# Key scales for the next head: eight loads of 256 KB spread over a head, in place of two of 1 MB

## The chip, the cores and the metric

The kernel runs on one core of one Trainium2 chip. The metric is the device time of one execution in microseconds (us). Before the change three runs took 1708.43, 1709.20 and 1712.97 us, a median of 1709.2 us. The profile comes from one further execution, which took 1714.34 us.

## The reference

The reference is one layer of gated cross attention followed by a gated feed-forward block, with quantisation simulated in both. Cut to what matters here:

```
q = LN(x) @ Wq + bq          # 2048 rows, 16 heads of 32
k, v = ctx @ Wkv + bkv       # 4096 rows
q, k: per row and head   round(x / s) * s,  s = max|x| / 127
v:    per column         round(v / s) * s
attn = softmax(q k^T / sqrt(32))           # 16 heads, 2048 x 4096
attn = round(attn / s) * s,  s = max(attn) / 255   # per row
x = x + tanh(g) * (attn @ v) @ Wp + ...
x = x + tanh(g2) * FFN(LN(x))              # 1.58-bit weights, 512 -> 2048 -> 512
```

All 2048 queries see all 4096 keys. Keys are held as integers, so each column of the score matrix has to be multiplied by its key's scale. These are the *key scales*: for each head one row of 4096 numbers.

## The kernel before, in words

There are three stages. In the first (to about 237 us) rows of x and ctx are normalised, projected and quantised, and the integers and scales go to DRAM: `q4d`, `k4d`, and `skd`, which holds the key scales as 16 rows of 4096 floats. The second stage is the attention loop (237 to 1454 us). The third is the feed-forward block.

**The loop.** A *unit* is one head and 128 queries, and there are 16 heads of 16 units, 256 in all (`steps`). For each unit:

- TensorE (PE) multiplies 128 queries by 4096 keys in three chunks of 1536, 1536 and 1024 (`scores`, L726).
- VectorE (DVE) multiplies each chunk by the key scales, writes it to one of three score buffers and takes the maximum (L735). The scales stand in the tile `skb`, 128 partitions of 4096 floats, every partition the same.
- GpSimd (POOL) makes the exponent's bias from the maximum (L750, L752). ScalarE (ACT) takes the exponential and rounds it to one byte per key (`exps`, L755); the result `r` has three buffers.
- The sync engine's queue (SP) issues a DMA that transposes `r` into `pT` (`turn_exps`, L769). POOL casts the transposed bytes to 16 bits (`rT<-pT`, L789), PE multiplies them by the values (L805), and ACT takes the product out (L816).

**Order.** Every engine runs its instructions in an order that the program writes out by hand (`manual_schedule`). One pass of the loop for unit i issues the scores of unit i, between them the exponentials of unit i-1 and whatever `plan` holds for the place (casts, value products and their loads), and at the end the transpose of unit i-2. After that transpose come the loads for the next head, so all of these stand in SP's one queue, behind and in front of the transposes.

**Loads for the next head.** A head needs three tiles: `kT` (its keys, from `k4d`), `skb` (from `skd`), `qT` (its queries, from `q4d`). Each has two buffers, so a head's tiles are filled while the head before runs. `load_piece(h, n)` issues one of eight pieces: n = 0, 1 are halves of `kT` and n = 4 to 7 quarters of `qT`, as transposing DMAs (L256); n = 2, 3 are halves of `skb`, 1 MB each, one 8 KB row of DRAM read once for each of 128 partitions (L249). In heads 1 to 13 piece n comes at unit 2n, so the scales come at units 4 and 6. In head 0 the places are in `LATE`: pieces 0 to 7 come at units 4, 6, 8, 10, 11, 12, 13 and 14. The last head's pieces are loaded at the start of the last 32 units, which alternate between two heads.

**Values.** For three of the four groups of heads, the values are projected inside the loop (`plan_group`, L652, started at units 3, 64 and 129): their inputs come by loads of 512 KB (`fx<-cTd`, L646), go out to DRAM (`vtd`, L674), come back in loads of 256 KB (`fx<-vtd`, L678) and are transposed (`vq<-fx`, L278). These also stand in SP's queue, mostly in heads 0 to 11.

Of the kernel before, what the change touches and what calls it, by code (L numbers as in the profile page):

```python
# [23 lines left out]
P = 128  # L24
# [9 lines left out]
def flamingo_kernel(  # L34
# [31 lines left out]
    nc = tc.nc  # L66
# [5 lines left out]
    H, HD = 16, 32  # L72
# [43 lines left out]
    KB = 512  # L116
    q4d = dram.tile([NQ, HPG * C], BF16, name="q4d")
    k4d = dram.tile([NK // HPG, HPG * C], BF16, name="k4d")
    skd = dram.tile([H, NK], F32, name="skd")
# [115 lines left out]
    heads = {}  # L235
# [3 lines left out]
    def load_piece(h, n):  # L239
        if h not in heads:  # L240
            heads[h] = (
                ah.tile([P, 1, NK // HPG], BF16, name="kT"),
                ah.tile([P, NK], F32, name="skb"),
                ah.tile([P, 1, NQ], BF16, name="qT"),
            )
        kT, skb, qT = heads[h]
        if n in (2, 3):
            a = (n - 2) * NK // 2
            nc.sync.dma_start(  # L249
                skb[:, a : a + NK // 2],  # L250
                skd[h : h + 1, a : a + NK // 2].broadcast_to([P, NK // 2]),
            )
            return
        dst, src, n = (kT, k4d, n) if n < 2 else (qT, q4d, n - 4)
        a = n * KB
        nc.sync.dma_start_transpose(  # L256
            dst[:, :, a : a + KB], src[a : a + KB, h * P : (h + 1) * P]
        )

    def value_scale(g, vmx):  # L260
# [48 lines left out]
    with tc.tile_pool(name="pw", bufs=1) as pw, tc.tile_pool(  # L309
# [79 lines left out]
        for t in range(QT - END):  # L389
            a = LEAD + 2 * t  # L390
# [159 lines left out]
        with tc.manual_schedule():  # L550
# [9 lines left out]
            n = len(order)  # L560
# [68 lines left out]

    VW = 256  # L630
    NV = NK // VW
    LATE = (4, 6, 8, 10, 11, 12, 13, 14)
    VALUES = {3: (1, 4, 2), 64: (2, 66, 0), 129: (3, 131, 0)}

    def plan_group(g, u0, dense):
# [76 lines left out]
    def scores(i, n):  # L712
        h, t = steps[i]
        kT, skb, qT = heads[h]
        if n == 0:
            live[i] = (
                scores_buffer(i),
                ar.tile([P, len(CHUNKS)], F32, name="m3"),
            )
        s, m3 = live[i]  # L720
        k0, w = CHUNKS[n]
        ps_s = asc.tile([P, CHUNKS[0][1]], F32, name="ps_s")
        for b in range(k0 // KB, (k0 + w) // KB):
            a, r = divmod(b, HPG)
            rows = slice(r * HD, (r + 1) * HD)
            nc.tensor.matmul(  # L726
                ps_s[:, b * KB - k0 : (b + 1) * KB - k0],
                qT[rows, 0, t * P : (t + 1) * P],
                kT[rows, 0, a * KB : (a + 1) * KB],
                start=True,  # L730
                stop=True,
                tile_position=(r * HD, 0),
            )

        nc.vector.tensor_tensor_reduce(  # L735
            s[:, k0 : k0 + w],
            ps_s[:, :w],
            skb[:, k0 : k0 + w],
            1.0,
            -3.0e38,  # L740
            ALU.mult,
            ALU.max,
            m3[:, n : n + 1],
        )

    def exps(i):
        h, t = steps[i]
        s, m3 = live.pop(i)
        m = ar.tile([P, 1], F32, name="m")
        nc.gpsimd.tensor_scalar(m, m3[:, 0:1], m3[:, 1:2], m3[:, 2:3], ALU.max, ALU.max)  # L750
        nb = ar.tile([P, 1], F32, name="nb")
        nc.gpsimd.tensor_scalar(nb, m, nsq[:, t, h : h + 1], LN255, ALU.mult, ALU.add)  # L752

        r = ar.tile([P, NK], U8, name="r")
        nc.scalar.activation(  # L755
            r.rearrange("p (n two) -> p two n", two=2),
            s.rearrange("p (two n) -> p two n", two=2),
            AF.Exp,
            bias=nb,
            scale=sq[:, t, h : h + 1],  # L760
            accum_out=rowsum[:, t, h : h + 1],
        )
        turning[i] = r

    def turn_exps(i):
        h, t = steps[i]
        if t % 2 == 0:
            heads["p", h, t // 2] = at.tile([P, 2, KT // 2, P], I16, name="pT", bufs=5)
        nc.sync.dma_start_transpose(  # L769
            heads["p", h, t // 2][:, t % 2, :, :],  # L770
            turning.pop(i).bitcast(I16),
        )
        if t % TG == TG - 1:
            plan_values(i, h, t // TG)
# [215 lines left out]
    def tiles(g):  # L990
        return range(g * GT, (g + 1) * GT)
# [421 lines left out]
    for j in range(8):  # L1413
        a = j * INNER // 8
# [43 lines left out]
    with tc.manual_schedule():  # L1458
        nc.vector.memset(less, -128.0 * INT_STEP)
        nc.vector.memset(ones_h, 1.0)  # L1460
        for i in range(len(steps)):
            h, t = steps[i]
            for n in range(len(CHUNKS)):
                scores(i, n)

                if n == 0 and i in VALUES:
                    plan_group(*VALUES[i])
                if n == 0 and i:
                    exps(i - 1)
                for run in plan.pop((i, n), ()):  # L1470
                    run()
            if i > 1:
                turn_exps(i - 2)
            if h == 0:
                if t in LATE:
                    load_piece(1, LATE.index(t))
            elif h + 2 < H and t % 2 == 0:
                load_piece(h + 1, t // 2)
            if 0 <= i - PAIR < TG:
                for n in ((0, 4, 2), (1, 3), (5,), (6, 7))[i - PAIR]:  # L1480
                    load_piece(H - 1, n)

        last = len(steps)

        def rest(i, n):
            return plan.pop((i, n), [])

        def run(fs_):  # L1490
            for f in fs_:
                f()

        def spreads_of(i, *engines):

            fs_ = [f for f in plan[i, 2] if isinstance(f, partial)]
            plan[i, 2] = [f for f in plan[i, 2] if not isinstance(f, partial)]
            return [partial(f, cast=e) for f, e in zip(fs_, engines)]

        act, pool = nc.scalar.copy, nc.gpsimd.tensor_copy  # L1500
        turn_exps(last - 2)
        exps(last - 1)
        turn_exps(last - 1)
        run(rest(last - 1, 3))
        for t in tiles(1):
            bias_x(t)
        take_second_head()
        take_scores()
        nc.gpsimd.memset(xis[1][:, :, C:], 0.0)
        for t in tiles(2):  # L1510
            load_x(t)
        run(rest(last, 1))
        run(rest(last + 1, 1))
        integers_x(0)
        for n in range(2, 8):
            first_project(2, n)
        wide_step(3)
        run(spreads_of(last, act, act))
        run(spreads_of(last + 1, pool, pool))
        for t in tiles(0):  # L1520
            turned_x(t)
            turned_x_out(t)
        residual_x(2)
        turned_steps(3)
        scale_o(3)
        take_bytes()
        for t in tiles(2):
            load_o(t)
        for t in tiles(3):
            load_x(t)  # L1530
        for name, v in (("lg", ln_g), ("lb", ln_b)):
            nc.sync.dma_start(vecs[name], row(v, INNER))
        steps_x(2)
        run(rest(last + 2, 1))
        run(spreads_of(last + 2, pool, pool))
        hidden(0, 0)
        run(rest(last + 3, 1))
        project(3)
        hidden(0, 1)
        quarter = spreads_of(last + 3, act, act)  # L1540
        run(rest(last + 3, 2))
        run(quarter[:1])
        residual_x(3)
        factors_x(1)
        integers_x(1)
        for t in tiles(2):
            bias_x(t)
        wide_step(4)
        hidden(1, 0)
        run(rest(last + 4, 1))  # L1550
        run(quarter[1:])
        run(spreads_of(last + 4, pool, pool))
        turned_steps(4)
        hidden(1, 1)
        scale_o(4)
        wide_step(5)
        run(rest(last + 5, 1))
        run(spreads_of(last + 5, act, act))
        project(4)
        turned_x(2)  # L1560
        turned_x_out(2)
        residual_x(4)
        gelu(0)
        turned_steps(5)
        scale_o(5)
        run(rest(last + 6, 1))
        project(5)
        gelu(1)
        bias_y(0)
        variance(0)  # L1570
        variance(1)
        factors_h(0)
        run(rest(last + 7, 1))
        run(rest(last + 7, 2))
        turned_x(3)
        residual_x(5)
        turned_x_out(3)
        factors_x(2)
        bias_y(1)
        for t in tiles(3):  # L1580
            load_o(t)
            bias_x(t)
        steps_x(3)
        take_rest()
        for k in range(2):
            nc.sync.dma_start_transpose(W2[k], w2q[:, k * INNER // 2 : (k + 1) * INNER // 2])
        for t in tiles(3):
            wide_step(t)
        for s in range(1, NGT - 2):
            turn(s)  # L1590
        last_turns()
# [32 lines left out]
```

## Time and profile before

| | |
|---|---|
| median of three runs | 1709.2 us |
| profiled execution, its own time | 1714.34 us |
| its span (first to last instruction) | 1712.5 us |
| attention loop in it | 236.7 to 1454.0 us |
| DVE busy over the span | 1566.7 us, 91% |
| ACT, POOL, PE busy | 1343.1, 1283.7, 1366.1 us |
| loads of key scales (L249) | 32 of 1024 KB |
| DMA busy, mean over the 16 engines, tenths | 9 in nearly every slice of the loop |

How to read it: busy times are of one execution. A group is named by line, engine, operation and tiles (out<-in). "Idle before" is time for which the engine stood still ahead of that group, with what ended it. SP does no arithmetic; its rows in the timeline are the time that it took to issue a DMA, and it takes the next only when that is done. The DMA share is the busy time of packets over that of 16 engines, and can pass 1 where packets overlap.

### The profile page before, as it was taken

To read this page: it belongs to the slowest core of one execution; us is meant where nothing else is said; L and a number is where in the kernel's file an instruction comes from. 1 tells how busy PE (TensorE), PEld (TensorE's weight loads), DVE (VectorE), ACT (ScalarE), POOL (GpSimd) and SP (SyncE) were. 2 spreads that over 40 slices of the span, in tenths; PEclk is the share of its full clock that TensorE was granted. 3 is DMA by queue.
4 is the path that set the end of the run, shared out by engine and by line. 5 is a ranking of instruction groups with operands and counts; after the bars stand their busy time and mean duration, and the time that the engine had idled before them with its cause. 6 is when DMAs were issued, how large, how long until landed. Compare 5 with 4: busy or idle time off the path is not lost. (4 is left out here: it accounts for less than half of the span.)

```text
span 1712.5 us, 31561 instructions
## 1 busy us (share of the span) xinstructions
PE 1366.1 (80%) x12174; PEld 592.1 (35%) x12174; DVE 1566.7 (91%) x2205; ACT 1343.1 (78%) x988; POOL 1283.7 (75%) x1315
## 2 busy tenths in 40 slices
PE   8999968889966899886678998766666577789986
PEld 4444423333322333332233333222222233434432
DVE  5787889999999999999989999999999989578998
ACT  2443468888889798888978888898887877679987
POOL 0001226889999899999988999999999998656645
PEclk9999975555555555555555556555555555889998
DMA  6767969999999999999999999989999776613325
GB/s 208 274 248 249 300 189 225 194 211 212 181 200 189 212 189 207 208 197 202 173 208 185 227 181 215 202 171 198 165 198 179 151 140 130 169 50 87 89 53 117
DMA packets 736331, 315.92 MB, mean 184 GB/s; under 512 B 658034, under 2 KB 703670, under 8 KB 729782
## 3 DMA queue, kind: packets, MB, share of 16 engines
q1 hardware_dynamic: 727414, 309.19, 83.4%
q10 hardware_dynamic: 8736, 4.72, 1.1%
q8 instruction: 95, 1.56, 0.4%
q14 instruction: 54, 0.44, 0.1%
q0 software_dynamic: 32, 0.01, 0.0%
HBM read 110.15 MB, written 40.12 MB: 88 GB/s over the span
## 5 line engine op out<-in xcount | busy, mean ns | idle before, releaser
L789 POOL CAST rT<-pT 128x2048 int16<-128x2048 uint8 x506 | 944.1, 1892 | 28.9 <-DMA pT<-r 7.5
L735 DVE CUSTOM_DVE_ANT_0 s<-ps_s,skb 128x1536 f32<-128x1536 f32 x531 | 806.0, 1574 | 21.1 <-PE ps_s L726 13.0
L755 ACT ACTIVATE r<-s,nb,sq 128x4096 uint8<-128x4096 f32 x177 | 673.1, 3803 | 135.6 <-POOL nb L752 77.1
L726 PE MATMUL ps_s<-kT,qT 32*128 32x512 bf16 x2048 | 463.7, 593 | 245.7 <-DVE m L735 232.1
L735 DVE CUSTOM_DVE_ANT_0 third<-ps_s,skb 128x1536 f32<-128x1536 f32 (+1 forms) x237 | 362.6, 1574 | 5.5 <-PE ps_s L726 3.2
L755 ACT ACTIVATE r<-third,nb,sq 128x4096 uint8<-128x4096 f32 x79 | 300.3, 3802 | 46.7 <-POOL nb L752 34.0
L726 PEld LDWEIGHTS <-qT 32*128 32x128 bf16 x2048 | 95.4, 99 | 578.0 <-issue 571.1
L805 PE MATMUL acc<-rT,vq 128*32 128x128 f16 x8192 | 265.1, 307 | 33.3 <-ACT o L816 25.2
L805 PEld LDWEIGHTS <-vq 128*32 128x32 f16 x8192 | 196.8, 137 | 147.0 <-issue 105.1
L652 PE MATMUL vacc<-fx 128*128 128x256 f32 x384 | 231.4, 706 | 7.7 <-ACT fx L661 6.7
L750 POOL TENSOR_SCALAR m<-m 128x1 f32<-128x1 f32 x256 | 91.8, 359 | 67.8 <-DVE m L735 61.2
L472 POOL TENSOR_SCALAR nsq<-sq 128x16 f32<-128x16 f32 x16 | 3.2, 203 | 171.9 <-DVE sq L291 171.9
L652 PEld LDWEIGHTS vacc<-fx 128*128 128x128 f32 x384 | 94.9, 306 | 91.3 <-issue 79.2
L431 PE MATMUL kacc<-wk_sb,cT 128*128 128x512 f32 x256 | 117.7, 603 | 0.0
L752 POOL TENSOR_SCALAR nb<-m,nsq 128x1 f32<-128x1 f32 x256 | 67.8, 265 | 23.9
L1117 PE MATMUL ph<-fx,skb 128*128 128x512 bf16 x256 | 64.2, 396 | 0.1
L431 PEld LDWEIGHTS kacc<-wk_sb,cT 128*128 128x128 f32 x256 | 47.1, 194 | 47.6 <-issue 47.0
L735 DVE DVE_READ_ACCUMULATOR2_ANT m<- 128x1 f32 x768 | 62.7, 82 | 0.0
L431 PE MATMUL qacc<-wq_sb,xT 128*128 128x512 f32 x128 | 59.4, 608 | 0.1
L460 DVE TENSOR_TENSOR f<-kacc,bk_sb 128x512 f32<-128x512 f32 x32 | 22.0, 689 | 31.1 <-PE kacc L431 30.1
L300 ACT COPY cT<-tr 128x512 f32<-128x512 f32 x32 | 18.6, 580 | 34.8 <-PE tr L299 34.6
L360 POOL TENSOR_SCALAR wi<-wt 128x512 bf16<-128x512 int32 (+1 forms) x32 | 21.7, 704 | 31.5 <-ACT wt L356 19.3
(233 smaller groups left out, 1370.1 us busy)
## 6 DMA issues: line engine op xcount, KB each, us to landing
skb<-skd SPq DMA_DIRECT2D x32, 1024.0 KB
fx<-cTd SPq DMA_DIRECT2D x48, 512.0 KB
wt<-in_L_ffn_w_dram SPq DMA_DIRECT2D x16, 1024.0 KB
in<-in_ctx_dram SPq DMA_DIRECT2D x32, 256.0 KB
cTd<-cT SPq DMA_DIRECT2D x8, 1024.0 KB
q4d<-rows4q SPq DMA_DIRECT2D x16, 512.0 KB
vtd<-fx SPq DMA_DIRECT2D x24, 256.0 KB
fx<-vtd SPq DMA_DIRECT2D x24, 256.0 KB
```

The lines of the kernel that those rows point to most:

```text
L360: nc.gpsimd.tensor_scalar(wi[:, a : a + w4], wt.bitcast(I32)[:, a : a + w4], 1.0, -1.0, ALU.min, ALU.max)
L431: nc.tensor.matmul(acc, tT[:, c, :], wk_sb[c] if kind == "k" else wq_sb[:, c, :], start=(c == 0), stop=(c == CC - 1),)
L460: nc.vector.tensor_tensor(f, acc, bk_sb, ALU.add)
L652: nc.tensor.matmul(state["acc"], wv_g[:, c, :], state["cT", j][:, c, :], start=(c == 0), stop=(c == CC - 1),)
L726: nc.tensor.matmul(ps_s[:, b * KB - k0 : (b + 1) * KB - k0], qT[rows, 0, t * P : (t + 1) * P], kT[rows, 0, a * KB : (a + 1) * KB], start=True,
L735: nc.vector.tensor_tensor_reduce(s[:, k0 : k0 + w], ps_s[:, :w], skb[:, k0 : k0 + w], 1.0, -3.0e38, ALU.mult, ALU.max, m3[:, n : n + 1],)
L750: nc.gpsimd.tensor_scalar(m, m3[:, 0:1], m3[:, 1:2], m3[:, 2:3], ALU.max, ALU.max)
L752: nc.gpsimd.tensor_scalar(nb, m, nsq[:, t, h : h + 1], LN255, ALU.mult, ALU.add)
L755: nc.scalar.activation(r.rearrange("p (n two) -> p two n", two=2), s.rearrange("p (two n) -> p two n", two=2), AF.Exp, bias=nb, scale=sq[: ...
L789: cast(spreads[k][:, 2 * u : 2 * u + 2, :, :] .bitcast(I16) .rearrange("p a (two b) q -> p a two (b q)", two=2), pTs[u][:, :, k * NW : (k ...
L805: nc.tensor.matmul(acc[c * HD : (c + 1) * HD, :], vq[:, kb, h % HPG * HD : (h % HPG + 1) * HD], rT[:, c, b, :], start=(k == 0 and b == 0), ...
L1117: nc.tensor.matmul(ph[:, n, :], xqT[:, c, tok], w1T[:, c, at : at + 512], start=(c == 0), stop=False,)
```

## The change

Two tables take the place of `LATE` and of the rule "piece n at unit 2n". The scales of the next head are loaded in eight pieces of 512 keys (256 KB: 2 KB for each of 128 partitions) by a new function `load_scales`; the pieces of `kT` and `qT` move forward to units 0, 2, 4, 6, 8 and 10. In head 0 everything comes four units later than in the others. The first head's tiles (loaded before the loop) and the last head's are loaded as before, in halves.

```diff
+    def load_scales(h, k):
+        a = k * KB
+        nc.sync.dma_start(
+            heads[h][1][:, a : a + KB], skd[h : h + 1, a : a + KB].broadcast_to([P, KB])
+        )
...
-    LATE = (4, 6, 8, 10, 11, 12, 13, 14)
+    PIECES_AT = {0: (0,), 2: (1,), 4: (4,), 6: (5,), 8: (6,), 10: (7,)}
+    SCALES_AT = {1: (0,), 3: (1,), 5: (2,), 7: (3,), 9: (4, 5), 10: (6,), 11: (7,)}
...
             if i > 1:
                 turn_exps(i - 2)
-            if h == 0:
-                if t in LATE:
-                    load_piece(1, LATE.index(t))
-            elif h + 2 < H and t % 2 == 0:
-                load_piece(h + 1, t // 2)
+            if h + 2 < H:
+                for n in PIECES_AT.get(t if h else t - 4, ()):
+                    load_piece(h + 1, n)
+                for k in SCALES_AT.get(t if h else t - 4, ()):
+                    load_scales(h + 1, k)
```

## The prediction

> **What bounds the kernel now.** I read the page first: which engine is busiest, and in which groups.
>
> ```profile
> PE 1366.1 (80%) x12174; PEld 592.1 (35%) x12174; DVE 1566.7 (91%) x2205; ACT 1343.1 (78%) x988; POOL 1283.7 (75%) x1315
> L735 DVE CUSTOM_DVE_ANT_0 s<-ps_s,skb 128x1536 f32<-128x1536 f32 x531 | 806.0, 1574 | 21.1 <-PE ps_s L726 13.0
> L789 POOL CAST rT<-pT 128x2048 int16<-128x2048 uint8 x506 | 944.1, 1892 | 28.9 <-DMA pT<-r 7.5
> ```
>
> DVE leads, and nearly all of it is the scaling of scores (L735). In the loop DVE runs from one chunk to the next; a unit takes 4.50 us where nothing disturbs it. So the loop can only gain what DVE stands idle. The second view is the table of windows, one per head (I cut at the start of each head's first chunk), of which these are heads 1, 4, 5, 8 and 9:
>
> ```profile
> core 0: us, PE busy (x) PEld busy (x) DVE busy (x) ACT busy (x) POOL busy (x), PEclk, DMA share, GB/s
> 313.50:390.50 77.00, 67.74 (x686) 28.32 (x686) 74.16 (x100) 64.98 (x42) 69.56 (x65) 0.50 1.05 201
> 539.90:618.70 78.80, 64.19 (x677) 27.54 (x675) 74.38 (x102) 64.65 (x42) 69.38 (x64) 0.50 1.02 207
> 618.70:692.90 74.20, 67.83 (x687) 28.62 (x686) 73.74 (x101) 63.31 (x42) 69.70 (x65) 0.50 1.00 200
> 842.60:924.50 81.90, 63.49 (x676) 27.03 (x673) 75.43 (x102) 66.06 (x45) 69.64 (x64) 0.50 0.99 199
> 924.50:998.50 74.00, 66.63 (x682) 28.77 (x682) 73.61 (x99) 64.23 (x39) 69.32 (x64) 0.50 1.05 205
> ```
>
> Length minus DVE busy is DVE's idle time: 2.8 us in head 1, 4.4 in head 4, 6.5 in head 8, but 0.5 and 0.4 in heads 5 and 9. Taken so for heads 0 to 13, the ones in which the change acts, the sum is 19.3 us: 5.8 in heads 0 and 1, 10.9 in heads 4 and 8, 2.6 in the other ten. That is the ceiling of any gain. The DMA share is about 1 throughout: DMA has little room, and a burst delays what is behind it.
>
> Third, what ended DVE's idle time in the loop (list of waits, DVE, us in total, times, longest):
>
> ```profile
> DVE s L735 <- PE ps_s L726: 13.0, 17, 3.1
> DVE s L735 <- ACT r L755: 5.5, 7, 1.9
> DVE vmx L671 <- ACT fx L661: 3.6, 3, 1.5
> ```
>
> PE itself is not short of time, so something holds it. The timeline of the worst place, head 8, shows it engine by engine (start, length, what; idle before it in brackets):
>
> ```profile
> 872.02 1.16 SPq L249 DMA_DIRECT2D skb<-skd  x1
> 873.28 6.48 SPq L769 DMA_TRANSPOSE pT<-r  x1
> ...
> 881.95 3.80 ACT L755 ACTIVATE r<-third,nb,sq 128x4096 uint8<-128x4096 f32 x1 [3.40 <-DMA pT<-r]
> ...
> 887.68 1.23 DVE L735 CUSTOM_DVE_ANT_0 s<-ps_s,skb 128x1024 f32<-128x1024 f32 x1 [3.08 <-PE ps_s L726]
> ...
> 881.97 1.89 POOL L789 CAST rT<-pT 128x2048 int16<-128x2048 uint8 x1 [3.08 <-DMA pT<-r]
> ...
> 886.05 1.05 PE L805 MATMUL acc<-rT,vq 128*32 128x128 f16 x32 [3.59 <-ACT o L816]
> ```
>
> A load of key scales is issued; the transpose behind it takes 6.48 us to issue instead of the usual 3.0 (median of L769). ACT waits 3.4 us for that transpose to free its buffer, POOL 3.1 us for its data, the value product on PE waits for ACT, the next scores stand behind it in PE's order, and DVE stands still for 3.1 us. The packets give the same: for four of those us the engines carry almost only 8 KB packets, some 36 in a us. One load keeps all 16 engines busy for 2.6 to 4.1 us.
>
> **The change part by part.**
>
> *Two loads of 1 MB go, eight of 256 KB come, in each of 14 heads.* The nearest row for the new load is L678, a load of the same 128 x 2 KB from DRAM; L249 is the old one (ns: shortest, median, longest issue):
>
> ```profile
> L249 SPq DMA_DIRECT2D skb<-skd x32: 332/576/1592, 226.8 to 1305.2; - x32
> L678 SPq DMA_DIRECT2D fx<-vtd x24: 424/530/999, 475.2 to 1155.4; - x24
> ```
>
> On the DMA engines: a packet of 2 KB takes 84 ns (median) against 315 for 8 KB; the 128 packets of one L678 load add up to 0.72 to 1.2 us of 16 engines, mostly 0.85. Eight make 6.8 us a head against 2 x 3.5 = 7.0 before. Engine work costs nothing more. On SP: 8 x 0.53 less 2 x 0.58, and 0.1 between any two issues, gives +3.7 us a head, 52 us in all. What hides it: SP's issues fill 1052 of the loop's 1217 us, and most of the rest it waits for ACT to finish r, about 10 us a head. Where that cover is thin (issues fill 70 of 73 us in head 12, 79 of 82 in head 8, and SP runs 4 to 8 us behind ACT from the middle of heads 3 and 7 into 4 and 8), the 3.7 us make it later. Bounds: 0 if the issue lies beside DMA work, which the transposes that stand blocked suggest; 3.7 us in each of heads 3, 7, 8 and 12, 15 us, if it all shows. Nearest to the first, because ACT and POOL can take a transpose some 5.5 us late before DVE stops (three r buffers): I take +2 us.
>
> The Trainium skill, "DMA: Bandwidth & Descriptors", section "Measured (HBM→SBUF, 128 partitions, SWDGE, issued from GpSimd)", says to batch to 1 MB or more, and its fit in "Anatomy of one DMA" is a fixed 2.0 us plus bytes over 436 GB/s. An estimate by it: 20.8 us for eight loads against 8.8 for two, 12 us more a head and 168 us over 14, were they run one at a time (the page's numbers are of DMAs issued by GpSimd; these come from SP). The L678 rows do show about 2.8 us from issue to last byte, so a wait of that kind is there, but the DMAs behind go on meanwhile, and this case's price is the 0.85 us above.
>
> *The burst goes.* A transpose now finds at most about 0.9 us in front of it (1.7 at unit 9) instead of 3.5. In heads 4 and 8 each of the two bursts made ACT wait 3 to 4 us, and the second came before the first was recovered (ACT recovers 4.50 - 4.0 = 0.5 us a unit). I expect DVE to lose 4 us there instead of 10.9, what is left coming from SP's lag at the end of heads 3 and 7: -7 us (bounds 0 and -10.9). In heads 0 and 1 ACT also waits for transposes right after the scale loads (1.7 and 2.6 us in head 0): -3 of 5.8 (bounds 0 and -5.8). In the ten others -1 of 2.6.
>
> *kT and qT pieces move.* The first three `qT` pieces come 4, 4 and 4 units earlier, at units 4, 6 and 8 instead of 8, 10 and 12, the last at 10 instead of 14. Six transposes of 1.25 us a head, same number, no cost of their own. Units 9 to 11 now carry four scale loads and a `qT` piece, about 3.5 us of DMA more than before; units 12 to 15 carry nothing, and let SP catch up for the next head. Free, unless SP is already late there (heads 3 and 7: 3 to 5 us late; +3 would reach the edge of 5.5). Its cost lies within the +2 and +15 above.
>
> *Waits that the change adds.* DVE's first unit of a head now waits for three loads per chunk rather than one; in heads 1 to 13 the last is issued at unit 11, four units ahead, so they are met. Not so out of head 0, where everything is four units later: the last scale load is issued at unit 15, behind the transpose of unit 13, and head 1's first unit needs it in its third chunk. Before, these were the places:
>
> ```profile
> 314.43 5.78 SPq L769 DMA_TRANSPOSE pT<-r  x2
> ...
> 316.88 1.22 DVE L735 CUSTOM_DVE_ANT_0 s<-ps_s,skb 128x1024 f32<-128x1024 f32 x1
> ```
>
> The first of those two transposes is issued by about 317.3; plus 2.8 us from issue to last byte is 320.1, against 316.88: DVE would wait 3.2 us, once. Behind it stand only head 1's next chunks, and PE, which waits for a free PSUM buffer. With ACT less behind in head 0 SP comes earlier; with its lag 2 us larger the wait is 5. Bounds 0 and 5; I take +2, because part of the wait is time that head 1 lost before anyway.
>
> Sum: -7 - 3 - 1 + 2 + 2 = **-7 us**. The profiled execution goes from 1714.3 to 1707.3. It was 5 us above the median of 1709.2, so in the runs I expect about 1702.5.
>
> **The rivals.**
>
> *Hidden anyway.* DVE's idle time moves rather than goes: heads 4 and 8 start with SP 5 to 8 us late because of the value loads in heads 3 and 7, and ACT then waits for transposes even without a burst. For it: heads 5 and 9 have the same two bursts and lose 0.5 us. Against: the wait chain at 872 to 888 us starts with the scale load. Then -4 in heads 4 and 8, -2 elsewhere, +2 and +2 back: about 1707.
>
> *Slower: SP's queue is the bound.* Heads 3, 7, 8 and 12 issue 32 scale loads instead of 8, 0.63 us each, on a queue that is 89 to 96% full there; when a queue this full gets 5% more, every transpose runs late and ACT waits unit after unit. It decides when SP's lag passes 5.5 us for longer than a few units, that is, when the 3.7 us do not fit into SP's idle time in heads 3 and 7. Against: transposes block on DMA, not SP, in the timeline. Then +15 for these heads and +4 at head 1, less 7: +12, about 1721.
>
> *Head 1 waits longer*, 5 us, and heads 4 and 8 gain as said: 1706.
>
> **How the numbers follow.** 0.3%, 5 us, is about what a measurement of this kernel can tell from no change. Forecast (gain of 5 to 14 us) 0.5; hidden anyway, or eaten by head 1's wait, 0.3; SP's queue 0.2, of which 0.03 within 0.3%. Faster 0.5, same 0.33, slower 0.17. The time is that of the likeliest, 1702.5. The low end is nearly the whole ceiling of 19.3 us less the two costs of 2: 1694. The high end takes in the smaller part of the slower case: 1715. For the likeliest alone, 1695 to 1704.
>
> **What would show it.** Right: no idle time of 3 us on DVE in heads 4 and 8, waits of ACT for pT well below 53.8 us, transposes with issues above 5 us gone from units 4 to 8, and a wait of DVE for a load at the third chunk of head 1. Wrong: SP later behind ACT in all heads, POOL waiting for pT at units 9 to 15, or L262's loads taking much over 0.55 us to issue or 0.9 us of the engines.

## The result, and the profile after

Slower, by 1.7%. Four runs of the changed kernel took 1734.69 to 1742.21 us, median 1740.49; four of the kernel before took 1708.43 to 1712.97, median 1710.85. The ratio is 1.0168, with a 95% interval of 1.0139 to 1.0197. The forecast was 1702.5 (1694 to 1715).

The profiled execution has a span of 1739.2 us, against 1712.5 before. The attention loop (236.2 to 1479.3 us) takes 1243.1 us instead of 1217.3: 25.8 of the 26.7 us are lost there. In the changed kernel line numbers from L262 on are higher by 6 or 7 (the scaling L735 is now L742, the exponentials L755 L762, the transposes L769 L776, the value products L805 L812). Of the page of the kernel after, these lines answer to those of before:

```profile
PE 1365.6 (79%) x12174; PEld 592.3 (34%) x12174; DVE 1567.0 (90%) x2205; ACT 1340.6 (77%) x988; POOL 1285.9 (74%) x1315
L742 DVE CUSTOM_DVE_ANT_0 s<-ps_s,skb 128x1536 f32<-128x1536 f32 x531 | 806.6, 1574 | 41.9 <-PE ps_s L733 22.4
L796 POOL CAST rT<-pT 128x2048 int16<-128x2048 uint8 x506 | 945.3, 1894 | 26.6 <-issue 5.8
L812 PE MATMUL acc<-rT,vq 128*32 128x128 f16 x8192 | 265.0, 307 | 47.2 <-ACT o L823 39.2
```

DVE works exactly as long as before (1567.0 against 1566.7 us): all that was lost is time in which DVE stood still. In the loop its idle time rises from 30.6 to 56.1 us, which is nearly all of the 25.8 us. Idle time ahead of the scaling (second line) went from 21.1 to 41.9 us. The table of windows of the kernel after, for heads 1, 4, 8 and 9, shows where:

```profile
core 0: us, PE busy (x) PEld busy (x) DVE busy (x) ACT busy (x) POOL busy (x), PEclk, DMA share, GB/s
313.67:394.62 80.95, 67.83 (x687) 28.71 (x686) 73.72 (x100) 62.95 (x42) 69.53 (x65) 0.50 1.00 198
547.41:630.19 82.78, 62.51 (x678) 26.80 (x676) 74.60 (x102) 64.89 (x43) 69.73 (x64) 0.54 1.06 196
855.15:937.14 81.99, 61.66 (x675) 26.61 (x673) 74.58 (x101) 65.93 (x43) 69.77 (x64) 0.52 0.97 194
937.14:1016.36 79.22, 67.34 (x683) 28.83 (x684) 73.90 (x99) 64.80 (x42) 69.68 (x64) 0.50 0.99 197
```

Length less DVE busy: 7.2 us in head 1 (2.8 before), 8.2 in head 4 (4.4), 7.4 in head 8 (6.5), 5.3 in head 9 (0.4). Heads 4 and 8, from which the gain was to come, lost too; and heads that had lost nothing lose now. Sorted by the unit in which DVE stands still, 15.8 of the 25.5 us more lie in the first unit of a head (6.9 in head 1, 9.0 in heads 2 to 14), the rest mostly in units 12 to 15. The list of waits of the kernel after, over the loop (us in total, times, longest), names three links of a chain and one wait apart:

```profile
ACT r L762 <- DMA pT<-r: 101.8, 53, 5.0
PE acc L812 <- ACT o L823: 39.2, 25, 3.5
DVE s L742 <- PE ps_s L733: 22.4, 25, 2.5
DVE s L742 <- DMA skb<-skd: 8.6, 2, 6.9
```

The first two of these in the kernel before:

```profile
ACT r L755 <- DMA pT<-r: 53.8, 28, 4.3
PE acc L805 <- ACT o L816: 25.2, 15, 4.7
```

ACT waits for transposes 101.8 us in 53 places; before it was 53.8 in 28. The second link was 25.2 us, the third 13.0 (shown in the prediction). The last row did not exist: 6.9 us of it are head 1's, the other 1.8 stand in the last two heads.

**Head 1.** The timeline of the kernel after at the start of head 1 (start, length, what):

```profile
304.61 1.85 SPq L776 DMA_TRANSPOSE pT<-r  x1
306.52 1.57 SPq L262 DMA_DIRECT2D skb<-skd  x2
308.19 0.38 SPq L681 DMA_DIRECT2D vtd<-fx  x1
308.66 0.55 SPq L653 DMA_DIRECT2D fx<-cTd  x1
309.30 4.94 SPq L776 DMA_TRANSPOSE pT<-r  x1
314.29 1.25 SPq L256 DMA_TRANSPOSE qT<-q4d  x1
315.60 1.47 SPq L262 DMA_DIRECT2D skb<-skd  x1
317.17 2.97 SPq L776 DMA_TRANSPOSE pT<-r  x1
320.19 0.58 SPq L262 DMA_DIRECT2D skb<-skd  x1
...
315.35 1.75 DVE L742 CUSTOM_DVE_ANT_0 s<-ps_s,skb 128x1536 f32<-128x1536 f32 x1
...
323.97 1.23 DVE L742 CUSTOM_DVE_ANT_0 s<-ps_s,skb 128x1024 f32<-128x1024 f32 x1 [6.86 <-DMA skb<-skd]
```

The last scale load of head 0 is issued at 320.19, and DVE's third chunk, which could have begun at 317.1, begins at 323.97, 3.2 us after the load's issue ended. One wait, 6.9 us.

**Crowded units.** SP's and the other engines' rows from the second half of head 12 to the start of head 13, in the timeline of the kernel after:

```profile
1215.90 2.59 SPq L776 DMA_TRANSPOSE pT<-r  x1
1218.54 1.53 SPq L262 DMA_DIRECT2D skb<-skd  x2
1220.11 1.23 SPq L1478 DMA_TRANSPOSE fx<-w1q  x1
1221.44 3.29 SPq L776 DMA_TRANSPOSE pT<-r  x1
1224.77 1.26 SPq L256 DMA_TRANSPOSE qT<-q4d  x1
1226.08 0.58 SPq L262 DMA_DIRECT2D skb<-skd  x1
1226.75 3.33 SPq L776 DMA_TRANSPOSE pT<-r  x1
...
1233.55 3.80 ACT L762 ACTIVATE r<-s,nb,sq 128x4096 uint8<-128x4096 f32 x1 [2.74 <-DMA pT<-r]
...
1244.92 0.24 ACT L823 COPY o<-acc 128x128 f32<-128x128 f32 x1
...
1245.22 1.04 PE L812 MATMUL acc<-rT,vq 128*32 128x128 f16 x32 [2.34 <-ACT o L823]
...
1246.84 1.22 DVE L742 CUSTOM_DVE_ANT_0 s<-ps_s,skb 128x1024 f32<-128x1024 f32 x1 [1.27 <-PE ps_s L733]
```

From one transpose to the next it is 5.54 us (1215.90 to 1221.44) and 5.31 us (to 1226.75), with no gap on SP, while DVE finishes a unit in 4.50. So SP falls behind by about a us a unit. (L1478 brings in weights of the feed-forward block; it stands there in both kernels. In the mean over heads 1 to 13 it is 6.4 us from the transpose of unit 8 to that of unit 9 and 5.0 to the next, where the kernel before has 4.8 and 3.7.) ACT, which needs the buffer that the transpose frees, waits 2.74 us at 1233.55 and is still late 11 us later; its copy of the value product ends at 1245.2, PE's next value product waits 2.34 us for that copy, the scores behind it in PE's order come late, and DVE stands still for 1.27 us. The same in every head, as means over heads 1 to 13 by unit (us; SP's lag is from the end of the exponentials to the issue of their transpose, ACT's from the end of the scaling to the start of the exponentials):

```
unit            0    1    2    3    4    5    6    7    8    9   10   11   12   13   14   15
SP,  before   2.1  2.5  1.5  1.3  2.7  2.6  3.1  3.4  2.1  2.5  1.7  2.4  1.8  1.9  1.4  2.0
SP,  after    1.8  3.2  2.9  3.3  3.0  3.9  3.3  3.7  4.1  5.7  5.9  5.1  2.8  1.2  1.0  1.6
ACT, before   1.1  1.1  1.3  1.7  1.3  1.1  1.9  2.1  2.1  1.7  1.5  1.9  1.2  1.0  1.0  1.3
ACT, after    1.6  1.1  1.0  1.7  1.5  1.6  1.7  2.1  1.4  1.5  1.5  2.1  2.9  3.5  3.2  3.2
```

A load that the tables place at unit u stands right in front of the transpose of unit u - 1. SP is latest at units 9 to 11, behind the four scale loads and the `qT` piece placed at units 9 to 11; ACT is late in units 12 to 15, after that; DVE loses at the next head's start. In head 12 ACT's lag is 4.8 us at unit 12 and 3.4 to 4.1 after it.

**Head 8, where the gain was to be.** Its bursts are gone, and the loss at the same place is not. Timeline of the kernel after:

```profile
891.24 0.54 SPq L653 DMA_DIRECT2D fx<-cTd  x1
891.88 5.05 SPq L776 DMA_TRANSPOSE pT<-r  x1
...
897.47 1.05 PE L812 MATMUL acc<-rT,vq 128*32 128x128 f16 x32 [2.54 <-ACT o L823]
...
899.10 1.23 DVE L742 CUSTOM_DVE_ANT_0 s<-ps_s,skb 128x1024 f32<-128x1024 f32 x1 [2.03 <-PE ps_s L733]
```

The load in front of the slow transpose is now one of 512 KB for the value projections, which was there before as well. DVE's wait at this place is 2.0 us instead of 3.1, in head 4 1.7 instead of 2.8.

### The profile page after: what moved, and what is told of

It is laid out like the page before. It is cut to its first block, busy times and chain, and to the rows that moved or that the text cites. A ratio compares the mean times of both kernels' runs of the same rounds, so it can differ in the third digit from the quotient of the medians.

```text
span 1739.2 us, 31694 instructions
## 1 busy us (share of the span) xinstructions
PE 1365.6 (79%) x12174; PEld 592.3 (34%) x12174; DVE 1567.0 (90%) x2205; ACT 1340.6 (77%) x988; POOL 1285.9 (74%) x1315
## 5 line engine op out<-in xcount | busy, mean ns | idle before, releaser
L742 DVE CUSTOM_DVE_ANT_0 s<-ps_s,skb 128x1536 f32<-128x1536 f32 x531 | 806.6, 1574 | 41.9 <-PE ps_s L733 22.4
L762 ACT ACTIVATE r<-s,nb,sq 128x4096 uint8<-128x4096 f32 x177 | 672.8, 3801 | 163.4 <-DMA pT<-r 79.1
L742 DVE CUSTOM_DVE_ANT_0 third<-ps_s,skb 128x1536 f32<-128x1536 f32 (+1 forms) x237 | 363.0, 1574 | 10.1 <-PE ps_s L733 8.2
L762 ACT ACTIVATE r<-third,nb,sq 128x4096 uint8<-128x4096 f32 x79 | 300.2, 3801 | 47.2 <-DMA pT<-r 22.7
L812 PE MATMUL acc<-rT,vq 128*32 128x128 f16 x8192 | 265.0, 307 | 47.2 <-ACT o L823 39.2
L812 PEld LDWEIGHTS <-vq 128*32 128x32 f16 x8192 | 196.9, 137 | 160.3 <-issue 103.0
L659 PE MATMUL vacc<-fx 128*128 128x256 f32 x384 | 230.9, 704 | 18.9 <-ACT fx L668 17.7
L659 PEld LDWEIGHTS vacc<-fx 128*128 128x128 f32 x384 | 94.8, 306 | 102.1 <-issue 76.5
L742 DVE DVE_READ_ACCUMULATOR2_ANT m<- 128x1 f32 x768 | 63.0, 82 | 0.0
L466 DVE TENSOR_TENSOR f<-kacc,bk_sb 128x512 f32<-128x512 f32 x32 | 22.0, 689 | 30.6 <-PE kacc L437 29.5
```

The costliest lines, as they stand in the source:

```text
L466: nc.vector.tensor_tensor(f, acc, bk_sb, ALU.add)
L659: nc.tensor.matmul(state["acc"], wv_g[:, c, :], state["cT", j][:, c, :], start=(c == 0), stop=(c == CC - 1),)
L742: nc.vector.tensor_tensor_reduce(s[:, k0 : k0 + w], ps_s[:, :w], skb[:, k0 : k0 + w], 1.0, -3.0e38, ALU.mult, ALU.max, m3[:, n : n + 1],)
L762: nc.scalar.activation(r.rearrange("p (n two) -> p two n", two=2), s.rearrange("p (two n) -> p two n", two=2), AF.Exp, bias=nb, scale=sq[: ...
L812: nc.tensor.matmul(acc[c * HD : (c + 1) * HD, :], vq[:, kb, h % HPG * HD : (h % HPG + 1) * HD], rT[:, c, b, :], start=(k == 0 and b == 0), ...
```

## Experiments

All of them are made on *stand-ins*; the transposing DMA itself was not changed in any run. In a stand-in each transposing DMA is replaced by a plain DMA that moves the same bytes on the same queue, for `pT`, `kT`, `qT` and the values in pieces of 256 bytes. The transposition is left out, so what is computed behind it is not the reference; the order of instructions on every engine is unchanged. The theories are these: **A**, the places are too full (units 9 to 11, and the end of head 0); **B**, the number of loads costs, wherever they stand; **C**, the moved `kT` and `qT` pieces cost. The ratio is always to the kernel before (the original one) on the same chip.

### 1. Stand-ins of both kernels: a queue with room

```diff
-        nc.sync.dma_start_transpose(
-            heads["p", h, t // 2][:, t % 2, :, :],
-            turning.pop(i).bitcast(I16),
+        nc.sync.dma_start(
+            heads["p", h, t // 2]
+            .rearrange("p u b c -> p (u b) c")
+            .rearrange("p (b u) c -> p u b c", u=2)[:, t % 2, :, :],
+            turning.pop(i).bitcast(I16).rearrange("p (b c) -> p b c", c=P),
         )
```

Stand-in of before:

> The kernel before with every transposing DMA (r to pT, kT, qT, values, feed-forward) replaced by a plain DMA that moves the same bytes from the same place to the same tile on the same queue, for pT, kT, qT and values in pieces of 256 bytes as the transposes do. The transposition itself is left out, so the output is not the reference's. It is the stand-in on which single causes are tried. If plain pieces of 256 bytes cost the DMA engines what transposed ones do (about 2 us for 512 KB), the loop keeps its 1217 us within 30 and SP's lag its pattern. If they are cheaper, SP and DMA have more room and the loop nears DVE's own 1186 us.

Stand-in of after:

> The changed kernel with the same replacement. Against its stand-in of before: theories A (four scale loads and a qT piece within units 9 to 11 make the transposes late) and B (84 more issues on SP's queue) both expect a loss again, 15 to 30 us, if the plain copies load DMA and SP as the transposes do; the wait of about 7 us at head 1's first unit, which depends on order alone, should stay in any case, so at least 4 us.

Measured, two runs each: 1693.69 us, ratio 0.9889 (0.9845 to 0.9932), for before; 1695.27, ratio 0.9898 (0.9836 to 0.9960), for after. The loss is gone but for one row, in the list of waits of the stand-in of after:

```profile
DVE s L746 <- DMA skb<-skd: 1.6, 1, 1.6
```

That is head 1's wait, 1.6 us instead of 6.9. A plain DMA keeps SP for 0.59 us (median) where the transpose takes 3.0; SP issues for 48% of the loop's time in the one and 60% in the other, instead of 87 to 89% in the originals, and its mean lag is 0.3 to 1.3 us in every unit. So neither eight loads, nor their places, nor the burst of 1 MB cost anything by themselves. They cost on a queue that is nearly full. (The DMA engines have more room there as well: their share over the loop is 0.80 in both, where the originals have 0.97 and 0.96. No run here holds the one and changes the other, so whether the queue or the engines behind it are short stays open.)

### 2. The same with the queue filled again

A second plain DMA of 128 KB behind each (from `r` to a scratch area in DRAM, 512 pieces of 256 bytes) makes ACT wait for SP about as late as the transpose did:

```diff
+        r16 = turning.pop(i).bitcast(I16).rearrange("p (b c) -> p b c", c=P)
...
-            turning.pop(i).bitcast(I16).rearrange("p (b c) -> p b c", c=P),
+            r16,
+        )
+        nc.sync.dma_start(
+            padd[i % 16], r16.rearrange("p (b e) c -> p e b c", b=PAD)[:, 0, :, :]
         )
```

> The stand-in of before (plain copies for the transposes, the transposition left out) with a second DMA behind each pT copy that moves a quarter of r (512 pieces of 256 bytes, 128 KB) to a scratch tensor in DRAM. It makes SP's queue heavier by what the plain copies are lighter than the transposes, about 14 us a head. Expected: SP about 2 us behind ACT on average as in the kernel before, DVE idle 15 to 35 us in the loop.

> The changed kernel with the same replacement and the same second DMA. If the loss comes from a queue that is nearly full (theory A: its units 9 to 11 overfull; theory B: more issues), it is back: 10 to 30 us slower than its stand-in of before, with SP's lag largest at units 9 to 11 (A) or larger by the same everywhere (B). If it is back nowhere but at head 1's first unit, the cause is something that only the transposes have.

Measured: 1706.06 us, ratio 0.9977 (0.9962 to 0.9993), and 1730.6 (two runs), ratio 1.0120 (1.0088 to 1.0152). SP issues for 86% of the loop in the stand-in of before. The loss is back: 24.5 us, 21.9 of it in the loop, SP's lag again greatest at unit 10 (4.6 us), and head 1's first unit waits 6.5 us for its scales. From here on "stand-in" means this filled one.

### 3. One part at a time

Eight loads, but at the places of the two (in heads 1 to 13 four at unit 4 and four at unit 6; pieces as before):

```diff
+            if 0 < h < H - 1:
+                for k in range(4):
+                    load_scales(h, 4 * (n - 2) + k)
+                return
```

> On the stand-in with the second DMA (its before lies 0.2% under the kernel before, its after 1.2% over it): eight loads of 256 KB, but four at unit 4 and four at unit 6 where the two of 1 MB stood (head 0: units 8 and 10); kT and qT pieces as before. Theory A (what costs is the place: four scale loads and a qT piece within units 9 to 11 make the transposes late, ACT is late at units 12 to 15, and the value product at the next head's unit 0 waits for ACT): within 6 us of the stand-in of before, no loss at unit 0. Theory B (what costs is 84 more issues on SP's queue): 15 to 22 us slower than the stand-in of before.

Two loads of 1 MB at units 4 and 6, the other pieces at their new places:

```diff
+    MOVED = {0: (0,), 2: (1,), 4: (2, 4), 6: (3, 5), 8: (6,), 10: (7,)}
...
```

> Same stand-in: two loads of 1 MB at units 4 and 6 as before, but in heads 1 to 13 the kT and qT pieces at units 0, 2, 4, 6, 8, 10 as in the changed kernel (a qT piece right behind each scale load). Theory A: 0 to 8 us slower than the stand-in of before, from more work at units 4 to 6. Theory B: within 3 us of it. Theory C (the move of the qT pieces is what costs): 15 us slower or more.

After, with head 0 as it was before:

```diff
             if h == 0:
                 if t in LATE:
                     load_piece(1, LATE.index(t))
-            elif h + 2 < H and t % 2 == 0:
-                load_piece(h + 1, t // 2)
+            elif h + 2 < H:
+                for n in PIECES_AT.get(t, ()):
+                    load_piece(h + 1, n)
+                for k in SCALES_AT.get(t, ()):
+                    load_scales(h + 1, k)
```

> Same stand-in: the changed kernel, but head 0 loads head 1's tiles as before (two loads of 1 MB, pieces at units 4 to 14). The wait of nearly 7 us at head 1's first unit goes; heads 0 and 1 gain the 5 us that they lost together in the profile, so 4 to 7 us less than the stand-in of after, 14 to 20 us over that of before. If the wait only took the place of later stalls: no gain.

The same, with the last three scale loads two units later, so that each unit has at most one load for the next head:

```diff
-    SCALES_AT = {1: (0,), 3: (1,), 5: (2,), 7: (3,), 9: (4, 5), 10: (6,), 11: (7,)}
+    SCALES_AT = {1: (0,), 3: (1,), 5: (2,), 7: (3,), 9: (4,), 11: (5,), 12: (6,), 13: (7,)}
```

> Same stand-in: as p4_head0, with the eight scale loads of heads 1 to 13 at units 1, 3, 5, 7, 9, 11, 12 and 13 instead of 1, 3, 5, 7, 9, 9, 10 and 11; the qT pieces stay at 4, 6, 8 and 10. Theory A: most of what is left of the loss goes, within 8 us of the stand-in of before, and SP's lag at units 9 to 11 falls from 4 to about 2.5 us. Theory B: as slow as p4_head0, since the number of loads is the same.

Measured, all four on one chip, which is that of experiment 6 too:

| | median, us | ratio (95%) | SP's lag, peak (unit) |
|---|---|---|---|
| eight loads at units 4 and 6 | 1719.9 | 1.0053 (1.0034 to 1.0073) | 4.6 (5) |
| pieces moved, two loads | 1709.3 | 0.9997 (0.9981 to 1.0012) | 3.9 (6) |
| after, head 0 as before | 1722.17 | 1.0072 (1.0042 to 1.0103) | 4.8 (10) |
| the same, loads spread | 1711.46 | 0.9996 (0.9979 to 1.0013) | 3.3 (12) |

C is out as the main cause, which was to cost 15 us or more, but moving the pieces is not free. It costs 0.2% by the stand-in of before of experiment 2 (0.9997 against 0.9977, on another chip) and 5.1 us by the one that experiment 6 ran on this chip (1709.3 against 1704.19 us; the two intervals do not meet). Two `qT` pieces then stand right behind a load of 1 MB, so this too may be crowding, at units 4 and 6. The third and fourth have the same loads in the same number and differ only in the places of three, and by 10.7 us: so B alone is out, and the crowding at units 9 to 11 is a real part. The first says it again at another place: four small loads in one unit are worse than one of 1 MB there, and the lag has its peak at the transpose right behind the second four.

### 4. One load in each unit

The spread table of experiment 3 has one load in each unit already. This one has too, with the `kT` and `qT` pieces back at their old places and head 0 as before, so that only the scale loads differ from before. If A is all, it should be as fast:

```diff
+    PIECES_AT = {0: (0,), 2: (1,), 8: (4,), 10: (5,), 12: (6,), 14: (7,)}
+    SCALES_AT = {1: (0,), 3: (1,), 4: (2,), 5: (3,), 6: (4,), 7: (5,), 9: (6,), 11: (7,)}
```

> Stand-in: head 0 as before; in heads 1 to 13 one load for the next head per unit at most: kT at units 0 and 2, scales of 256 KB at 1, 3, 4, 5, 6, 7, 9 and 11, qT at 8, 10, 12 and 14. Theory A (crowding is what costs, not the number of loads): SP's lag stays below 3 us in the mean at every unit, and the time is that of the stand-in of before or up to 6 us less, since its two bursts are gone. Theory B (the number): 8 us or more slower than the stand-in of before.

Measured: 1717.4 us, ratio 1.0046 (1.0025 to 1.0067), although SP's lag stays between 1.3 and 3.2 us. A alone is out too: it is 0.7% more than the stand-in of before of experiment 2, of which the loop shows 6 us (1215.6 against 1209.5), and 0.9% more than that of experiment 6. Both ran on other chips than this, so the size is uncertain, but the number costs something after all.

### 5. The last link: value products later in PE's order

If DVE stops only because PE's value product waits for ACT in front of the next scores, putting the products of the first 224 units behind the third chunk of scores should give DVE more room:

```diff
-            plan[i + 5 + k, 1].append(partial(products, k))
+            late = 2 if i + 5 + k < PAIR else 1
+            plan[i + 5 + k, late].append(partial(products, k))
```

In the stand-in of after, of before, and of experiment 4:

> The stand-in of after, with each value product on PE placed behind the third score chunk of its unit instead of behind the second (in the first 224 units). Theory: ACT's lateness reaches DVE because PE's value product waits for ACT to empty its only accumulator, with the next scores behind it in PE's order; one chunk later PE has 1.7 us more. Then DVE's idle time in heads 2 to 13 (21 us in the stand-in of after) falls by a third or more and the time by 5 to 12 us. If ACT's lateness reaches DVE by another way (score buffers): no change within 3 us, or slower.

> The same move of the value products in the stand-in of before. Its stalls in heads 1, 4 and 8 end with the same wait of PE for ACT, so 2 to 6 us less than the stand-in of before if the theory is right; no change or slower if the move delays ACT's copies and the values as much as it gains.

> p4_one with the value products moved behind the third chunk as well: if both theories hold, the fastest of the stand-ins, 5 to 12 us below the stand-in of before (what DVE still loses in heads 0 to 13 there is 14 us).

Measured: 1750.9 us, ratio 1.0242 (1.0221 to 1.0262); 1743.31, ratio 1.0196 (1.0178 to 1.0213); 1746.87, ratio 1.0215 (1.0197 to 1.0233). All are misses: 20 to 37 us slower instead of faster. In the first, DVE stands still for 4.8 to 6.1 us in each of the heads with value projections (1, besides its one wait, 2, 4 to 6 and 8 to 10) and not at all in heads 12 and 13: there the product of the projection (L659) already stands behind the third chunk, and with two products there the next unit's first scores come late. The move puts in a stall of its own, so it does not test the link. That link rests on the timelines alone.

### 6. The parts beside the whole, on one chip

Head 0 alone as in after, the others as before:

```diff
...
             if h == 0:
-                if t in LATE:
-                    load_piece(1, LATE.index(t))
+                for n in PIECES_AT.get(t - 4, ()):
+                    load_piece(1, n)
+                for k in SCALES_AT.get(t - 4, ()):
+                    load_scales(1, k)
```

> The stand-in of the kernel before, with head 0 alone as in the kernel after (eight loads, the last at unit 15); heads 1 to 13 as before. As in the other stand-ins the transposition is left out. If head 0's places are a part of the loss by themselves, it loses what the stand-in of the kernel after gained when head 0 was put back: 8 us over the stand-in of before, of which 5 to 7 us is one wait of DVE at head 1's first unit, and heads 2 to 13 stay as they were. If the places in head 0 cost only together with the crowding in the later heads, it loses under 4 us.

And three kernels from above once more:

> The stand-in of the kernel before once more, on the chip of its neighbours, as the base of the sums: 0.997 to 1.000 of the kernel before.

> The stand-in of the kernel after once more: 24 us over the stand-in of before, 1.010 to 1.015 of the kernel before. If the parts add up, it equals the loss of head 0's places plus that of the crowded units 9 to 11 plus that of the number of loads.

> Eight loads spread, with head 0 as before, once more, beside the stand-in of before. If the number of loads costs nothing when they are spread, the two agree within 0.3%; if SP's extra issues cost by themselves, it is 4 to 9 us slower, as the kernel with one load in each unit was.

| | median, us | ratio (95%) | over the stand-in of before |
|---|---|---|---|
| stand-in of before | 1704.19 | 0.9956 (0.9940 to 0.9971) | |
| head 0 alone | 1709.15 | 0.9979 (0.9965 to 0.9992) | +5.0 us |
| loads spread, head 0 as before | 1711.2 | 1.0002 (0.9988 to 1.0016) | +7.0 us |
| stand-in of after | 1721.54 | 1.0062 (1.0046 to 1.0079) | +17.4 us |

The list of waits of the kernel with head 0 alone shows its 5 us as one wait:

```profile
DVE s L748 <- DMA skb<-skd: 6.0, 1, 6.0
```

The other part is in ACT's waits for SP's queue. First the stand-in of before, then that with spread loads, then that of after:

```profile
ACT r L761 <- DMA pad<-r: 41.6, 29, 3.3
```

```profile
ACT r L769 <- DMA pad<-r: 60.4, 41, 4.1
```

```profile
ACT r L768 <- DMA pad<-r: 75.4, 50, 4.0
```

Experiment 3 ran on the same chip, and what ran in both agrees: the kernel before took 1711.03 and 1711.54 us, the spread loads 1711.46 and 1711.2. So its kernels can be set against the same 1704.19:

| | over the stand-in of before |
|---|---|
| pieces moved, two loads | +5.1 us |
| eight loads at units 4 and 6, pieces as before | +15.7 us |
| after, head 0 as before | +18.0 us |

The parts do not add up. Head 0's places cost 5.0 us by themselves, but on top of the crowding nothing: 17.4 us with them, 18.0 without. (The 8 us by which experiment 3's kernel lies under the stand-in of after in experiment 2 are a difference between two chips.) Head 1's wait of 6.0 us seems to take the place of later stalls. Eight loads, spread, and the moved pieces cost 7.0 us together; how much of it is the number alone these runs do not tell. Putting three of the eight where the change has them adds some 11 us (18.0 against 7.0), and this crowding is the largest part. Expected of the stand-in of after was 24 us over before; it was 17.4, so the whole differs between chips, and each part is known to some 4 to 6 us.

## Why the prediction was wrong

**"The burst goes": -7, -3 and -1 us.** This step failed first. Its mechanism was half right. Transposes that took over 5 us to issue went from 25 to 13 in heads 0 to 13; those right behind a scale load from 15 to 1, those right behind a load for the values from 9 to 12. But all the transposes of these heads together took 704 us to issue instead of 713: 9 us less, while SP's issues in all grew by 43 us. And the gain on DVE was missing: head 8 lost 7.4 us instead of 6.5, head 4 8.2 instead of 4.4, head 0 3.8 instead of 3.0. At the very places, about 1.1 us was won in each; the 512 KB loads of the value projections make the same slow transpose. The chain was read as starting with the scale load, because that stood in front; the rival "hidden anyway" was right on this. Besides, the 6.5 us of head 8 were not a fixed quantity: the same stand-in of before lost 6.4 us in head 8 on one chip and 2.6 on another.

**SP's issues: +3.7 us a head, taken as +2 in all.** The amount was right (43 us measured, 52 estimated); what it costs was not, and this is the step that failed most dearly. The prediction took the issues to be hidden in the some 10 us a head for which SP waits for ACT, everywhere but in heads 3, 7, 8 and 12. They were not: SP's lag at units 9 to 11 rose from 2.2 to 5.6 us in the mean of heads 1 to 13, by nearly the whole 3.7, and the units without loads in which SP caught up, 12 to 15, came too late for it. So the ten heads that had lost 2.6 us in sum lose 16.6, heads 4 and 8 lose 4.7 more instead of 7 less, and heads 0 and 1 lose 5.2 more.

The other support, "ACT and POOL can take a transpose some 5.5 us late before DVE stops", is not refuted: the largest lag in units 8 to 11 is 5.2 to 7.7 us in each of heads 1 to 13 (1.2 to 4.5 before). The 5.5 were reached in ten of these 13 heads, where the text expected it in heads 3 and 7 at most. What comes behind was not in the text: PE's value product waits for ACT to empty the accumulator, and the next scores stand behind it. ACT's lag at unit 14 of a head and DVE's idle time in the next head's first unit (us, heads 2 to 14 in order, kernel after) show how little lateness of ACT it takes:

```
ACT's lag at unit 14 of the head before   3.1 4.1 2.1 1.8 2.6 3.2 3.5 4.3 4.2 2.9 3.3 3.4 2.6
DVE idle in the head's first unit         0.6 1.7 0.0 0.0 0.2 1.0 1.1 0.3 0.0 1.0 1.5 1.3 0.4
```

Where ACT lags 2.1 us or less, nothing is lost; from 2.6 on mostly 0.2 to 1.7. (Heads 9 and 10, with over 4 us and little lost here, had lost 1.0 and 2.5 us a unit earlier.) The lag is 0.9 where nothing disturbs it. The margin of this last link is thus some 1.7 us. It counts ACT's lateness, not that of the transposes, and so does not stand against the 5.5. That reading is from the trace; the runs that were to test it did not.

**"kT and qT pieces move": free.** Alone it cost 5.1 us on the stand-in on one chip, and 0.2% between two (experiment 3). And the text saw that units 9 to 11 now carry four scale loads and a `qT` piece and let that pass, because it looked only at heads that were late before. Every head becomes late there: two consecutive units of SP's queue take 6.4 and 5.0 us in the mean against DVE's 4.50, and that, not the issue time summed over a head, is what had to be compared. (Before, single units took up to 5.7 us, but the next one made up for it.) It cost some 11 us on the stand-in.

**Head 1's wait: +2, bounds 0 and 5.** The place and the kind were right; it was 6.9 us. The estimate of 3.2 took a last load issued at 317.3, where SP stood in the trace of before; it was issued from 320.19 to 320.77, because the two units before it, from the transpose at 304.61 to that at 317.17, kept SP for 12.6 us where DVE needs 9: three scale loads, a `qT` piece and two transfers of the values stand there. Taking 2 for a worked-out 3.2 was without ground.

**The rivals and the range.** The slower rival named the right engine, with 0.17, and gave 1721. It was too small as it let the loss come in four heads and not in all, and took off the 7 us of the burst. The observations named as signs of a mistake came: SP later behind ACT in units 1 to 12 of heads 1 to 13, and L262's loads at 0.78 us to issue in the mean (0.58 in the median) where 0.55 was the mark. POOL's wait for pT, also named, did not come (4.9 us against 7.5). The rule to batch to 1 MB or more, in the Trainium skill's "DMA: Bandwidth & Descriptors", section "Measured (HBM→SBUF, 128 partitions, SWDGE, issued from GpSimd)", pointed the right way here. The estimate of 12 us a head, which the prediction did not follow, did not come about: all 14 heads together lost 26 us, and on a queue with room (experiment 1) 1.6. Two figures of the prediction were misread, without weight in its sum: SP's issues fill 1061 us of the loop before and not 1052, and 315 ns for a packet of 8 KB is the median over the whole execution, where in the loop it is 381.

## What to carry to other kernels

Compare a queue unit by unit with the pace of the engine that bounds the kernel: what counts is whether the issues of one unit fit into one unit, not their sum over a head, and a queue that, like this one, is 87% full has little to spare at a place with three extra issues. Follow a late engine to the one that bounds the kernel: here, by the timelines, through a single accumulator, emptied by ACT and standing in PE's order ahead of the next scores, which let ACT be only about 1.7 us later than usual. Compare parts of a change on one chip, against the same base. Before a gain is booked on a wait that a large transfer ends, see whether the next thing in the same queue would end it as late.

## What the runs showed of the hardware that was not expected

- A transposing DMA of 512 KB keeps SP for 3.0 us in the median (1.3 to 6.9); a plain DMA of the same bytes in 256-byte pieces keeps it for 0.59 us. What comes right behind that one takes long instead: a second plain DMA of 128 KB 2.4 to 2.5 us. In the stand-in of after of experiment 1 a load of 256 KB takes 2.39 us to issue right behind such a copy (median of 84) and 0.58 right behind another scale load (14). So SP's time for a DMA goes largely by what stands ahead of it in the queue.
- Four loads of 256 KB one after another delayed the queue more than one of 1 MB in the same place (SP's lag 4.6 us against 2.2 to 2.3 at unit 5), and the kernel took 15.7 us more on the same chip, although they move the same bytes.
- The time that the same kernel loses at one place varies: the stand-in of after was 1.2% above the kernel before on one chip (two runs) and 0.6% on another (six), each with an interval of about 0.3% or less to either side.
